# Rows for the expert blocks: four quarter gathers a block against one whole gather with a trip through DRAM

## The chip, the cores and the metric

The kernel runs on one core of one Trainium2 chip. The metric is the device time of one execution in microseconds (us), the median of the runs shown. Durations inside the kernel come from one profiled execution; times within it count from the start of its span.

The engines are named as in the profile: PE (TensorE; its weight loads are PEld), DVE (VectorE), ACT (ScalarE), POOL (GpSimd) and SP (SyncE, which here only starts DMAs).

## The reference, cut to what matters

Input x is 8 x 256 rows of 512 numbers, 2048 rows in all. A first layer (layer norm, a long convolution by head, a weighting with `ctx_2048`, a residual) yields a new x. The second layer is a mixture of experts, and the change is in how it gets its rows:

```
xf = layernorm(x).reshape(2048, 512)
scores = sigmoid(xf @ gate_w.T)                       # 8 experts
topk_w, topk_idx = top_k(scores, 2)
topk_w = topk_w / topk_w.sum() * 2.5
shared_out = (silu(xf @ shared_wg.T) * (xf @ shared_wu.T)) @ shared_wd.T
h = silu(xf @ exp_wg[e].T) * (xf @ exp_wu[e].T)       # 352 wide, per expert e
all_out[e] = h @ exp_wd[e].T
out = x + shared_out + sum over the 2 picked experts of topk_w * all_out[e]
```

Each row needs two experts of eight, so the kernel computes only those 4096 pairs of row and expert.

## The kernel before, in words

**First stage.** 16 tiles of 128 rows pass through the convolution (a loop over 32 pairs of heads). Beside it run the shared expert's products, as `steps` called one by one, and the routing by chunks of four tiles. The normed rows are stored to the DRAM tensor `xn_d` (L342). The residual tiles `x2` get the shared expert's output and go to `out` by SP (L757).

**Routing into a table.** For every chosen pair a row number and a gate are scattered to a table in DRAM, sorted by expert (L661). `load_table` brings it back as `tab` (L893). One-hot products on PE then pick out the table's column for each block: `slots` (L931) for whole blocks and `half_slots` (L948) for half blocks. Their results become the row numbers `row` (for scattering results), the gates `gate`, and the gather indices `src` and `src_h`.

**Blocks.** The pairs are cut into 34 blocks of 128 rows that always run: 26 "pure" ones of one expert, and 8 "mixed" ones whose two halves of 64 rows belong to two experts (from position 7 of the sequence on, every third). 16 further half blocks stand behind a branch (L1358, after block 6 is prepared) and do not run with these inputs.

For a block b, in order of its data:

- `gather(b)` (L1180) issues four indirect DMAs on POOL. DMA c fetches, for the 32 rows of chunk c, each row's four quarters of 128 numbers into four groups of 32 partitions of `xg`. So the quarters come to lie as `block_T` needs them. `xg` has four buffers.
- `block_T(b)` (L1213) is one transpose on DVE by 32x32 squares, `xg` to `xT`.
- `block_up` (L1257): PE multiplies by the expert's gate and up weights `wgu_sb` (loaded by SP at L1138); ACT and DVE form h.
- `block_hT` (L1300): transposes of 32-row pieces on DVE, 16 for each block, to `hTb`.
- `block_down` (L1315): PE multiplies by the down weights `wd_sb`; ACT scales by the gate into `ys` (three buffers, L1332), and POOL scatters the block with addition into `out` (`send`, L1336). A mixed block sends its first half at once; the second half is put into `late` and sent by `send_late` later. Sends add to the same tensor, so each waits until the one before has landed.

**Order.** The order is written by hand; every engine runs its instructions in program order. Gathers of the first four blocks are issued before the last four steps of the shared expert (L1229). Then the memory of the shared expert is released, and SP loads the down weights `wd_sb` into it (L1244, L1247), in two pieces for each of 8 experts; the first of these loads waits for the last stores of `x2`. PE's first down product needs expert 0's two pieces. In the main loop (L1368), turn k loads the expert number of block k+2, transposes block k+2, gathers block k+4, computes `block_up` and `block_hT` of block k and `block_down` of block k-2.

Around the table's return, two copies (L917) lay its columns out by quarters, on DVE and on ACT; the quarter products (L937, L955, L962) use them.

Of the kernel before, what the change touches and what calls it, by code (L numbers as in the profile page):

```python
# [8 lines left out]
F32 = mybir.dt.float32  # L9
I32 = mybir.dt.int32  # L10
AF = mybir.ActivationFunctionType
ALU = mybir.AluOpType
# [3 lines left out]
P = 128  # L16
B, D, L = 8, 256, 512
# [4 lines left out]
NTOK = NT * P  # L22
# [3 lines left out]
TC = TPC * P  # L26
# [24 lines left out]
HP = P // 2  # L51
# [18 lines left out]
def tile_xattn_moe(  # L70
# [29 lines left out]
    V, G, A, T, S = nc.vector, nc.gpsimd, nc.scalar, nc.tensor, nc.sync  # L100
# [63 lines left out]
    for e in range(NEXP):  # L164
# [6 lines left out]
        out=upper,  # L171
# [605 lines left out]
    def g(name, s, dtype=F32):  # L777
        return const.tile(s, dtype, name=name)
# [102 lines left out]
    def load_table():  # L881
# [20 lines left out]
                )  # L902
        return tab


    row = g("row", [P, NBLK + NMIX], I32)
    gate = g("gate", [P, NBLK])
    src = g("src", [P, NQ, NPURE], I32)
    src_h = [g(f"src_{n}", [P, 2, NHALF - n * NCOND], I32) for n in range(2)]
    by_quarter = []  # L910

    def turn_quarters(f, tab, copy):
        own = const.tile([P, TC], F32, name="rows_by_quarter") if f == 0 else shp.tile(
            [P, TC], F32, tag="sg", name="gates_by_quarter", bufs=2
        )
        by_quarter.append(own.rearrange("p (c q b) -> p c q b", c=NQ, q=NQ))
        copy(  # L917
            by_quarter[f],
            tab[:, :, f]
            .rearrange("p (c b) -> p c b", b=Q)  # L920
            .unsqueeze(2)
            .to_broadcast([P, NQ, NQ, Q]),
        )

    def lay_rows(to, ps, name, at=slice(0, P)):

        spare = g(name, [P, to.shape[1]])
        V.tensor_scalar(spare[at], ps, 0.0, lane[at], ALU.is_equal, ALU.mult)
        V.scalar_tensor_tensor(to, ps, float(NTOK), spare[at], ALU.add, ALU.add)

    def slots(tab, pick):  # L931

        ps = ps_tp.tile([P, 2 + NQ, NPURE], F32, tag="tp", name="slots_ps")
        for f in range(2):
            T.matmul(ps[:, f, :], lhsT=tab[:, :, f], rhs=pick, start=True, stop=True)
        for c in range(NQ):
            T.matmul(  # L937
                ps[:, 2 + c, :],
                lhsT=by_quarter[0][:, c].rearrange("p q b -> p (q b)"),
                rhs=pick,  # L940
                start=True,
                stop=True,
            )
        V.tensor_scalar(src, ps[:, 2:], float(NQ), behind, ALU.mult, ALU.add)
        lay_rows(row[:, :NPURE], ps[:, 0, :], "spare")
        V.tensor_copy(gate[:, :NPURE], ps[:, 1, :])

    def half_slots(any_half, first_half):  # L948

        ps = ps_tp.tile([P, 2, NQ, NHALF], F32, tag="tp", name="halves_ps")  # L950
        for f in range(2):
            quarter = [by_quarter[f][:, c].rearrange("p q b -> p (q b)") for c in range(NQ)]
            for c in range(2):
                for n in range(2):
                    T.matmul(  # L955
                        ps[:, f, c],
                        lhsT=quarter[2 * n + c],
                        rhs=any_half[:, n],
                        start=(n == 0),
                        stop=(n == 1),  # L960
                    )
                T.matmul(  # L962
                    ps[:, f, 2 + c, :NMIX],
                    lhsT=quarter[2 + c],
                    rhs=first_half,
                    start=True,
                    stop=True,
                )
        rows_h = g("rows_h", [P, NHALF])
        for n, m in enumerate((NHALF, NMIX)):  # L970
            two, cols = slice(2 * n, 2 * n + 2), slice(NPURE, NPURE + m)
            V.tensor_scalar(
                src_h[n], ps[:, 0, two, :m], float(NQ), behind, ALU.mult, ALU.add
            )
            for c in range(2):
                A.copy(rows_h[c * Q : (c + 1) * Q, :m], ps[c * Q : (c + 1) * Q, 0, 2 * n + c, :m])
                at = slice((2 * n + c) * Q, (2 * n + c + 1) * Q)
                A.copy(gate[at, cols], ps[at, 1, 2 * n + c, :m])
            at = slice(0, HP)
            to = slice(NPURE + n * NHALF, NPURE + n * NHALF + m)  # L980
            lay_rows(row[at, to], rows_h[at, :m], f"spare_{n}", at)


    def first_of_all(t):
# [33 lines left out]
    behind = const.tile([P, 1], F32, name="behind")  # L1018
    for q in range(NQ):
        G.memset(behind[q * Q : (q + 1) * Q], float(NTOK * NQ + q))  # L1020

    todo = iter(steps)
    done = 0
# [130 lines left out]
    settle()  # L1154
    for n in range(3):
        step()
        if n == 2:
            turn_quarters(0, tab, V.tensor_copy)
            turn_quarters(1, tab, A.copy)
        settle()  # L1160
    slots(tab, pick)
    half_slots(any_half, first_half)
# [8 lines left out]
    def send_late():  # L1171
        while late:
            send, *half = late.pop()
            send(*half)


    def rows_in(b):
        return P if b < NSURE else HP

    def gather(b):  # L1180
        xgs[b] = (rows if b < NSURE else spare).tile([P, NQ, P], F32, tag="xg", name=f"xg_{b}")
        for c in range(rows_in(b) // Q):
# [3 lines left out]
            G.indirect_dma_start(  # L1186
                out=xgs[b][:, c, :],
                out_offset=None,
                in_=xn_q,
                in_offset=bass.IndirectOffsetOnAxis(ap=at[:, c % at.shape[1], i : i + 1], axis=0),  # L1190
                bounds_check=(NTOK + P) * NQ - 1,
                oob_is_err=True,
            )

    def load_ek(b):
# [119 lines left out]
    def block_down(k):  # L1315
        if k < NSURE:
            ps = ps_b.tile([P, L], F32, tag="dn", name=f"y_{k}")
        else:
            ps = ps_spare.tile([P, 2, L], F32, tag="up", name=f"y_{k}")[:, 0]
        hT = hTb.pop(k)  # L1320
        for ft, (_, fw) in enumerate(F_TILES):
            for at, e in eks[k]:
                T.matmul(  # L1323
                    ps[at],
                    lhsT=hT[:fw, ft].rearrange("p c b -> p (c b)")[:, at],
                    rhs=weights(wd_sb, k, e, ft * L, L)[:fw],
                    start=(ft == 0),
                    stop=(ft == NF - 1),
                )
        y = (blk if k < NSURE else spare).tile([P, L], F32, tag="y", name=f"ys_{k}")  # L1330
        n = rows_in(k)
        A.activation(y[:n], ps[:n], AF.Copy, scale=gate[:n, k : k + 1])  # L1332


        def send(at, col):
            G.indirect_dma_start(  # L1336
                out=out,
                out_offset=bass.IndirectOffsetOnAxis(
                    ap=row[: at.stop - at.start, col : col + 1], axis=0
                ),  # L1340
                in_=y[at],
                in_offset=None,
                bounds_check=NTOK + P - 1,
                oob_is_err=True,
                compute_op=ALU.add,
            )

        send(eks[k][0][0], k)
        if len(eks[k]) > 1:
            late.append((send, slice(HP, P), k + NHALF))  # L1350

    more = nc.values_load(
        used[0:1, 0:1], min_val=2 * NPURE, max_val=2 * NPURE + NHALF,
# [122 lines left out]
```

## Time and profile before

| | us |
|---|---|
| median of 3 runs (806.08 to 808.03) | 807.78 |
| the profiled execution | 806.57 |
| its span | 804.9 |
| PE busy | 765.0 (95%) |
| DVE busy | 526.1 (65%) |
| POOL busy | 472.1 (59%) |
| ACT busy | 201.0 (25%) |
| table back in SBUF, first slot product | 485.5 |
| first up product of the blocks | 517.4 |
| first down product of the blocks | 531.7 |
| last product of PE ends | 781.4 |
| last send issued by POOL | 795.0 |

In the profile, a line of a timeline reads: start, duration, engine, line of the source, operation, output<-inputs, shapes, count; in brackets stands how long the engine sat idle before it, and what ended that. A line of the groups reads: count, then busy us and the mean ns of one, then idle us before them with the releasers. "issue" means that nothing the profile shows was waited for. In the slices, a digit is the busy share of 1/40 of the span in tenths. A matmul of 32-bit numbers appears twice in a count. A table of stages gives for each stretch its length, PE's busy time and number of matmuls, the granted clock of PE as a share of full speed, the DMA engines' share and GB/s.

### The profile page before, as it was taken

To read this page: it belongs to the slowest core of one execution; us is meant where nothing else is said; L and a number is where in the kernel's file an instruction comes from. 1 tells how busy PE (TensorE), PEld (TensorE's weight loads), DVE (VectorE), ACT (ScalarE), POOL (GpSimd) and SP (SyncE) were. 2 spreads that over 40 slices of the span, in tenths; PEclk is the share of its full clock that TensorE was granted. 3 is DMA by queue.
4 is the path that set the end of the run, shared out by engine and by line. 5 is a ranking of instruction groups with operands and counts; after the bars stand their busy time and mean duration, and the time that the engine had idled before them with its cause. 6 is when DMAs were issued, how large, how long until landed. Compare 5 with 4: busy or idle time off the path is not lost. (4 is left out here: it accounts for less than half of the span.)

```text
span 804.9 us, 8780 instructions
## 1 busy us (share of the span) xinstructions
PE 765.0 (95%) x2539; PEld 341.8 (42%) x2539; DVE 526.1 (65%) x1199; ACT 201.0 (25%) x387; POOL 472.1 (59%) x477
## 2 busy tenths in 40 slices
PE   9999999999999999999999998999999999999770
PEld 4333334433334433334434445455544544554330
DVE  3678868767558767658654372198877777676630
ACT  2222342543342543341422101011111111111110
POOL 7877785289175289175240035737677777777531
PEclk9999999999999999999999998999999999999895
DMA  7585433333504333412101951394333343334333
GB/s 248 181 286 168 151 117 118 117 47 111 170 33 125 117 46 112 138 33 92 52 14 59 416 178 44 109 298 83 60 60 69 64 67 62 58 70 67 59 40 39
DMA packets 51892, 88.13 MB, mean 109 GB/s; under 512 B 8832, under 2 KB 24192, under 8 KB 50688
## 3 DMA queue, kind: packets, MB, share of 16 engines
q1 hardware_dynamic: 37120, 61.77, 23.9%
q0 software_dynamic: 10400, 17.87, 12.9%
q10 hardware_dynamic: 4320, 7.87, 2.8%
q8 instruction: 24, 0.39, 0.2%
q14 instruction: 28, 0.23, 0.1%
HBM read 65.81 MB, written 21.66 MB: 109 GB/s over the span
## 5 line engine op out<-in xcount | busy, mean ns | idle before, releaser
L415 PE MATMUL cv<-kv,tz 128*64 128x512 f32 (+2 forms) x720 | 190.5, 607 | 0.2 <-POOL kv L375 0.2
L1186 POOL DMA_INDIRECT xg<-xn_d,src x136 | 138.6, 1019 | 55.5 <-issue 37.8
L1263 PE MATMUL up<-wgu_sb,xT 128*128 (+3 forms) x672 | 166.8, 460 | 3.1 <-DVE x L756 1.4
L687 PE MATMUL gu<-xfT,wsh 128*128 128x512 f32 x352 | 157.1, 600 | 1.2 <-issue 1.2
L375 POOL TENSOR_TENSOR kv<-vT,ctxT 128x512 f32<-128x512 f32 x128 | 133.1, 1073 | 18.4 <-issue 10.1
L1307 DVE STREAM_TRANSPOSE hTb<-h 32x96 f32<-32x96 f32 (+1 forms) x528 | 137.9, 261 | 7.9
L1263 PEld LDWEIGHTS up<-wgu_sb,xT 128*128 128x128 f32 (+1 forms) x672 | 97.0, 170 | 77.1 <-issue 33.4
L415 PEld LDWEIGHTS cv<-kv,tz 128*64 128x64 f32 (+2 forms) x720 | 60.9, 150 | 119.8 <-issue 97.8
L687 PEld LDWEIGHTS gu<-xfT,wsh 128*128 128x128 f32 x352 | 67.5, 193 | 85.8 <-issue 84.3
L1323 PE MATMUL y<-wd_sb,hTb 128*128 (+5 forms) x252 | 96.5, 608 | 6.8 <-DVE hTb L1307 5.4
L1336 POOL DMA_INDIRECT out_dram<-ys,row x42 | 65.5, 1560 | 63.5 <-issue 32.3
L477 DVE TENSOR_TENSOR prod<-cv,ctxT 128x1024 f32<-128x1024 f32 x64 | 78.2, 1221 | 16.4 <-PE cv L415 14.8
L661 POOL DMA_INDIRECT table<-entries,to x32 | 31.6, 987 | 90.5 <-DVE at L657 81.9
L486 DVE TENSOR_REDUCE convT<-prod 128x128 f32<-128x1024 f32 x64 | 78.1, 1220 | 2.2
L731 PE MATMUL dn<-wshd,hT 128*128 128x512 f32 x160 | 70.2, 593 | 0.0
L1323 PEld LDWEIGHTS y<-wd_sb,hTb 128*128 128x128 f32 (+3 forms) x252 | 35.8, 173 | 54.5 <-issue 43.3
L701 ACT ACTIVATE sg<-gu 128x512 f32<-128x512 f32 (+1 forms) x24 | 14.3, 596 | 162.8 <-PE gu L687 149.1
L531 POOL TENSOR_TENSOR skip<-ctxT,w 128x512 f32<-128x512 f32 x16 | 17.3, 1081 | 59.3 <-ACT w L523 30.1
L1332 ACT ACTIVATE ys<-y,gate 128x512 f32<-128x512 f32 x34 | 23.4, 687 | 109.4 <-DMA out_dram<-ys,row 62.4
L1271 ACT ACTIVATE h<-up 128x352 f32<-128x352 f32 x34 | 15.7, 463 | 138.1 <-PE up L1263 138.1
L415 PE MATMUL cv<-kv,td 128*128 128x512 f32 x88 | 47.2, 619 | 0.0
L1218 DVE STREAM_TRANSPOSE xT<-xg 128x512 f32<-128x512 f32 x34 | 24.1, 710 | 34.4 <-DMA xg<-xn_d,src 26.1
(188 smaller groups left out, 618.6 us busy)
## 6 DMA issues: line engine op xcount, KB each, us to landing
tz<-in_toep_dram SPq DMA_DIRECT2D x32, 384.0 KB, 3.4
wgu_sb<-in_egu_dram SPq DMA_DIRECT2D x8, 1408.0 KB, 15.4
ctxT<-in_cT_dram SPq DMA_DIRECT2D x16, 384.0 KB, 4.6
x<-in_xv_dram SPq DMA_DIRECT2D x16, 256.0 KB, 3.5
x<-in_x_dram SPq DMA_DIRECT2D x16, 256.0 KB, 4.7
xn_d<-xn ACTq DMA_DIRECT2D x16, 256.0 KB, 2.3
out_dram<-x SPq DMA_DIRECT2D x16, 256.0 KB, 2.5
wd_sb<-in_ed_dram SPq DMA_DIRECT2D x8, 512.0 KB, 10.0
```

The lines of the kernel that those rows point to most:

```text
L375: G.tensor_tensor(kv[:, mb], vT[t][:, at, :, cols].unsqueeze(2).to_broadcast([P, B, NH, NH]), ctxT[t][:, at, :, cols].unsqueeze(3).to_broa ...
L415: T.matmul(banks[lb][cols], lhsT=w, rhs=x, start=first, stop=left[lb][here[0]] == 0,)
L477: V.tensor_tensor(prod, ps.rearrange("p k b j i -> p (k b) j i"), ctxT[t][:, 2 + 2 * n : 4 + 2 * n, :, cols] .rearrange("p k b i -> p (k b ...
L486: V.tensor_reduce(convT[t][:, two, :, cols].rearrange("p k b j -> p (k b) j"), prod, AX.X, ALU.add)
L661: ins = G.indirect_dma_start(out=table, out_offset=bass.IndirectOffsetOnAxis(ap=to[:, i : i + 1], axis=0), in_=entry[:, i, n, :], in_offse ...
L687: T.matmul(ps, lhsT=wsh[:, k, m0 : m0 + m], rhs=rhs[k], start=(k == 0), stop=(k == NLB - 1))
L731: T.matmul(ps, lhsT=hTs[c][:, ft, i * P : (i + 1) * P], rhs=wshd[:, ft, :], start=(ft == 0), stop=False,)
L1186: G.indirect_dma_start(out=xgs[b][:, c, :], out_offset=None, in_=xn_q, in_offset=bass.IndirectOffsetOnAxis(ap=at[:, c % at.shape[1], i : i ...
L1263: T.matmul(ps[at, m, :FF], lhsT=xTs[k][:, j].rearrange("p c b -> p (c b)")[:, at], rhs=weights(wgu_sb, k, e, (m * NLB + j) * FF, FF), star ...
L1307: V.transpose(hT[q * Q : (q + 1) * Q, :n, c], hk[c * Q : (c + 1) * Q, q * NF * Q : (q * NF + n) * Q].rearrange("p (t a) -> p t a", a=Q),)
L1323: T.matmul(ps[at], lhsT=hT[:fw, ft].rearrange("p c b -> p (c b)")[:, at], rhs=weights(wd_sb, k, e, ft * L, L)[:fw], start=(ft == 0), stop= ...
L1336: G.indirect_dma_start(out=out, out_offset=bass.IndirectOffsetOnAxis(ap=row[: at.stop - at.start, col : col + 1], axis=0), in_=y[at], in_o ...
```

## The change

- `gather` issues one indirect DMA on POOL: 128 whole rows of 2 KB into a new SBUF tile `picked` (one buffer). SP then writes `picked` to a DRAM tile of its own, and brings it back into `xg` by four DMAs, one for each quarter. All five are on SP's queue.
- The gathers are issued two blocks earlier: three more before the down weights are loaded (one after each of three of the last four steps), and in the main loop turn k gathers block k+6, from turn 1 on.
- `send_late` is no longer called inside `gather`, only after it.
- The table is no longer laid out by quarters. The row numbers come from `tab` itself; the half blocks' products have 64 columns of the table as weights and write 64 partitions. `src`, `src_h`, `rows_h` and `behind` go; the second halves' row numbers get a tile of their own. `slots` has 2 products instead of 6, `half_slots` 7 instead of 12, and the 8 small ACT copies become copies on DVE.

The rest of the program and its order are the same. The diff, cut to what the text speaks of:

```diff
    def slots(tab, pick):
-    ps = ps_tp.tile([P, 2 + NQ, NPURE], F32, tag="tp", name="slots_ps")
+    ps = ps_tp.tile([P, 2, NPURE], F32, tag="tp", name="slots_ps")
     for f in range(2):
         T.matmul(ps[:, f, :], lhsT=tab[:, :, f], rhs=pick, start=True, stop=True)
-    for c in range(NQ):
-        T.matmul(
-            ps[:, 2 + c, :],
-            lhsT=by_quarter[0][:, c].rearrange("p q b -> p (q b)"),
-            rhs=pick,
-            start=True,
-            stop=True,
-        )
-    V.tensor_scalar(src, ps[:, 2:], float(NQ), behind, ALU.mult, ALU.add)
     lay_rows(row[:, :NPURE], ps[:, 0, :], "spare")
     V.tensor_copy(gate[:, :NPURE], ps[:, 1, :])
...
+    halves = [slice(n * HP, (n + 1) * HP) for n in range(2)]
+    for f in range(2):
+        for n in range(2):
+            T.matmul(
+                ps[halves[0], f],
+                lhsT=tab[:, halves[n], f],
+                rhs=any_half[:, n],
+                start=(n == 0),
+                stop=(n == 1),
+            )
+    for at, f, to in ((1, 0, 0), (1, 1, 1), (0, 0, 2)):
         T.matmul(
+            ps[halves[at], to, :NMIX],
+            lhsT=tab[:, halves[1], f],
+            rhs=first_half,
             start=True,
             stop=True,
         )
...
-        if n == 2:
-            turn_quarters(0, tab, V.tensor_copy)
-            turn_quarters(1, tab, A.copy)
...
    def gather(b):
-    xgs[b] = (rows if b < NSURE else spare).tile([P, NQ, P], F32, tag="xg", name=f"xg_{b}")
-    for c in range(rows_in(b) // Q):
-        if c == 3:
-            send_late()
-        at, i = (src, b) if b < NPURE else (src_h[c // 2], b - NPURE)
-        G.indirect_dma_start(
-            out=xgs[b][:, c, :],
-            out_offset=None,
-            in_=xn_q,
-            in_offset=bass.IndirectOffsetOnAxis(ap=at[:, c % at.shape[1], i : i + 1], axis=0),
-            bounds_check=(NTOK + P) * NQ - 1,
-            oob_is_err=True,
-        )
+    n = rows_in(b)
+    own = rows if b < NSURE else spare
+    picked = own.tile([P, L], F32, tag="picked", name=f"picked_{b}", bufs=1)
+    G.indirect_dma_start(
+        out=picked[:n],
+        out_offset=None,
+        in_=xn_d,
+        in_offset=bass.IndirectOffsetOnAxis(ap=row[:n, b : b + 1], axis=0),
+        bounds_check=NTOK + P - 1,
+        oob_is_err=True,
+    )
+    picked_d = dram.tile([n, L], F32, name=f"picked_d_{b}")
+    S.dma_start(out=picked_d, in_=picked[:n])
+    xgs[b] = own.tile([P, NQ, P], F32, tag="xg", name=f"xg_{b}")
+    for q in range(NQ):
+        S.dma_start(
+            out=xgs[b][q * Q : (q + 1) * Q, : n // Q],
+            in_=picked_d[:, q * P : (q + 1) * P].rearrange("(c b) m -> b c m", b=Q),
+        )
...
 for k in range(TPC):
     step()
     settle()
     if k <= AHEAD:
         block_T(seq[k])
+        gather(seq[k + AHEAD + 2])
...
-        if k + AHEAD + 2 < NSURE:
-            gather(seq[k + AHEAD + 2])
+        if 0 < k < NSURE - AHEAD - 4:
+            gather(seq[k + AHEAD + 4])
         send_late()
```

More of the change, by code (lines that the diff above doesn't have):

```diff
@@ L903, in load_table @@
         return tab
-    row = g("row", [P, NBLK + NMIX], I32)
+    row = g("row", [P, NBLK], I32)
+    second_row = g("second_row", [HP, NMIX], I32)
     gate = g("gate", [P, NBLK])
[L908 to L914, printed above, removed]
-        )
[L916 to L922, printed above, removed]
-        )
     def lay_rows(to, ps, name, at=slice(0, P)):
@@ L931, in slots, with half_slots @@
     def slots(tab, pick):
-        ps = ps_tp.tile([P, 2 + NQ, NPURE], F32, tag="tp", name="slots_ps")
+        ps = ps_tp.tile([P, 2, NPURE], F32, tag="tp", name="slots_ps")
         for f in range(2):
             T.matmul(ps[:, f, :], lhsT=tab[:, :, f], rhs=pick, start=True, stop=True)
-        for c in range(NQ):
+        lay_rows(row[:, :NPURE], ps[:, 0, :], "spare")
+        V.tensor_copy(gate[:, :NPURE], ps[:, 1, :])
+    def half_slots(any_half, first_half):
+        ps = ps_tp.tile([P, 3, NHALF], F32, tag="tp", name="halves_ps")
+        halves = [slice(n * HP, (n + 1) * HP) for n in range(2)]
[9 more added lines that the diff above has]
+        for at, f, to in ((1, 0, 0), (1, 1, 1), (0, 0, 2)):
             T.matmul(
-                ps[:, 2 + c, :],
-                lhsT=by_quarter[0][:, c].rearrange("p q b -> p (q b)"),
-                rhs=pick,
+                ps[halves[at], to, :NMIX],
+                lhsT=tab[:, halves[1], f],
+                rhs=first_half,
                 start=True,
@@ L943, in slots @@
             )
-        V.tensor_scalar(src, ps[:, 2:], float(NQ), behind, ALU.mult, ALU.add)
[L945 to L954, printed above, removed]
-                    T.matmul(
[L956 to L965, printed above, removed]
-                    start=True,
-                    stop=True,
-                )
-        rows_h = g("rows_h", [P, NHALF])
-        for n, m in enumerate((NHALF, NMIX)):
[L971 to L981, printed above, removed]
+        for n, m in enumerate((NHALF, NMIX)):
+            at, cols = halves[n], slice(NPURE, NPURE + m)
+            lay_rows(row[at, cols], ps[at, 0, :m], f"spare_{n}", at)
+            V.tensor_copy(gate[at, cols], ps[at, 1, :m])
+        lay_rows(second_row, ps[halves[0], 2, :NMIX], "spare_2", halves[0])
     def first_of_all(t):
@@ L1016, in tile_xattn_moe @@
     G.memset(first_block[:, 0:1], float(P - 1))
-    behind = const.tile([P, 1], F32, name="behind")
-    for q in range(NQ):
-        G.memset(behind[q * Q : (q + 1) * Q], float(NTOK * NQ + q))
     todo = iter(steps)
@@ L1332, in block_down, with send @@
         A.activation(y[:n], ps[:n], AF.Copy, scale=gate[:n, k : k + 1])
-        def send(at, col):
+        def send(at, index, col):
             G.indirect_dma_start(
@@ L1338, in send @@
                 out_offset=bass.IndirectOffsetOnAxis(
-                    ap=row[: at.stop - at.start, col : col + 1], axis=0
+                    ap=index[: at.stop - at.start, col : col + 1], axis=0
                 ),
@@ L1346, in send @@
             )
-        send(eks[k][0][0], k)
+        send(eks[k][0][0], row, k)
         if len(eks[k]) > 1:
-            late.append((send, slice(HP, P), k + NHALF))
+            late.append((send, slice(HP, P), second_row, k - NPURE))
     more = nc.values_load(
```

## The prediction

> **What bounds the kernel now.** I read the page first (slices, costliest groups), then the timelines of PE, POOL and SP from 480 us on, the clock by stage, and the order of instructions in both programs. TensorE is busy 765.0 of 804.9 us; that hides that in the blocks' stage POOL sets the pace.
>
> ```profile
> PE   9999999999999999999999998999999999999770
> POOL 7877785289175289175240035737677777777531
> ...
> L1186 POOL DMA_INDIRECT xg<-xn_d,src x136 | 138.6, 1019 | 55.5 <-issue 37.8
> L1336 POOL DMA_INDIRECT out_dram<-ys,row x42 | 65.5, 1560 | 63.5 <-issue 32.3
> ```
>
> A tenth of 7 on POOL looks like slack. POOL's timeline at the end shows that it is none: the gaps between its DMAs are the 0.30 us that follows every one of them.
>
> ```profile
> 751.36 1.60 POOL L1336 DMA_INDIRECT out_dram<-ys,row  x1 [1.77 <-issue]
> 753.27 1.05 POOL L1186 DMA_INDIRECT xg<-xn_d,src  x1 [0.31 <-DVE h L1275]
> 754.63 1.00 POOL L1186 DMA_INDIRECT xg<-xn_d,src  x1 [0.31 <-issue]
> 755.94 1.01 POOL L1186 DMA_INDIRECT xg<-xn_d,src  x1 [0.31 <-issue]
> 757.25 1.01 POOL L1186 DMA_INDIRECT xg<-xn_d,src  x1 [0.30 <-issue]
> ...
> 764.18 1.45 POOL L1336 DMA_INDIRECT out_dram<-ys,row  x1 [3.99 <-ACT ys L1332]
> 768.15 1.43 POOL L1336 DMA_INDIRECT out_dram<-ys,row  x1 [2.52 <-DMA out_dram<-ys,row]
> 772.60 1.56 POOL L1336 DMA_INDIRECT out_dram<-ys,row  x1 [3.02 <-DMA out_dram<-ys,row]
> ...
> 789.41 1.56 POOL L1336 DMA_INDIRECT out_dram<-ys,row  x1 [4.03 <-DMA out_dram<-ys,row]
> 794.98 1.56 POOL L1336 DMA_INDIRECT out_dram<-ys,row  x1 [4.01 <-issue]
> ```
>
> Three blocks (two whole, one mixed with two sends) take POOL 24.8 us (sends at 726.57 and 751.36), PE 22.3 (up at 623.81 and 646.10). POOL falls 2.5 us behind in every three. Each send also waits for the one before to land: 5.57 us apart with 128 rows, 4.2 on average with 64 (764.18, 768.15, 772.60). So the last send starts at 794.98 though PE is done at 781.4, and the span ends 9.9 us after that send. PE pays too:
>
> ```profile
> 531.73 2.74 PE L1323 MATMUL y<-wd_sb,hTb 128*128 128x512 f32 x6
> ...
> 749.42 2.74 PE L1323 MATMUL y<-wd_sb,hTb 128*128 x6
> 757.60 4.61 PE L1323 MATMUL y<-wd_sb,hTb 128*128 x6 [5.43 <-DVE hTb L1307]
> ```
>
> DVE waits for a late gather, hTb is late, PE stands 5.43 us and then runs at half clock (4.61 for 2.74). With 1.05 and 0.23 us of waits a little earlier, POOL's lag costs PE 5.43 + 1.87 + 1.28 = 8.6 us.
>
> The other place is SP's queue before the blocks:
>
> ```profile
> 506.99 10.74 SPq L757 DMA_DIRECT2D out_dram<-x  x4
> 521.02 0.40 SPq L1244 DMA_DIRECT2D wd_sb<-in_ed_dram  x1
> ```
>
> The down weights (wd) start once the last residual store has landed, 3.6 us after its issue at 517.4. The first expert's two pieces need 4.8 more (the second goes out 0.5 later, 4.3 us minimum to landing), so at 525.8 they are there; PE wants them at 531.73. Slack: 6 us.
>
> **The change, part by part.**
>
> *Table stage.* Gone: the two 128x512 copies, the quarter products, the 8 small ACT copies. 18 products become 9: 485.50 to 490.81 now, 9 at 0.23 us (slots_ps to its quarters: 0.47 for two) is 2.1, so 3.2 us less on PE. The granted clock (column after PE's busy time and count) is half here, after 2.4 us of idling and these tiny products:
>
> ```profile
> 488.00:489.00 1.00, 1.00 (x8) 0.58 0.00 0
> ...
> 495.00:496.00 1.00, 1.00 (x4) 1.00 0.01 0
> ```
>
> If it stays full, up to 5.4 us are saved; if the same stretch stays slow, 2.1. I take 3.7. PE would reach the first down product at 528.0. The row numbers are ready at 486.7 (tab 485.45, two products, two DVE operations) instead of 487.7.
>
> *The gathers on POOL.* 136 become 34. At 1.31 us with their gap, three a block are gone: 3.9 us of 8.2 per block. A 2 KB-row gather is in no row; on POOL it lies between 1.01 (quarter) and 1.56 (the send, same shape). Either leaves POOL well below PE.
>
> *The trip.* Each block now goes gather, write to DRAM, four reads, and there is one buffer `picked`, so the next gather waits for this write. Cycle c = gather + write + about 0.2 of hand-over. The write has a twin: ACT's store of xn and SP's reads of it follow by 2.06 us (419.58 to 421.64). The gather's landing lies between 2.6 us (64 KB quarter) and 4.8 (send, 256 KB read, added and written). I take 3.6, nearer the quarter because nothing is added: c = 5.9, bounds 4.9 and 7.1 (estimates from these rows). Four reads take SP 1.75 to issue and 3.3 to land.
> [...]
>
> *What queues behind it on SP.* Five blocks' trips stand ahead of the first two residual stores, seven ahead of wd. Gather 6's write lands at 486.7 + 7c; reads and stores issue to x15 2.2, landing and wait 3.6, first expert 4.8: PE gets wd at 497.3 + 7c = **538.6**, against 531.7 before. PE stands from 528.0 to 538.6, so all of the table stage's saving is spent waiting. The wait brings half clock: the trace's case (757.6 to 761.9 slow, so 4.3 us at half speed) costs 2.1. PE is **9.0 us late** here. Bounds: c 4.9 gives 531.6 (+2.0 with slow clock), c 7.1 gives 547.0 (+17.4).
> [...]
>
> *First blocks after it.* wd's 16 issues are held to 13.9 us (521.0 to 534.9), so block 7's write issues at 547.7 and lands like wd's pieces, 10.1 later: 557.8. POOL is in order: gather 8 waits for that write, and send 0 stands behind gather 8, at 559.3; its result is ready at 544.1. Lag 15 us. ys has three buffers: ys 3 needs send 0 landed (564.7), y 3 ends at 565.5, so PE does not feel it. DVE transposes xg 7 (landed 561.4) when hT 4 is done, about 561. Then POOL gains: with c at 6.4 beside the sends, three blocks take 6.4 + 6.4 + 7.4 (late send: 1.3 + 4.2 + 1.9) = 20.2 against PE's 22.3. Seven whole blocks first win 7 x (7.3 - 6.4) = 6.4, the branch at block 6 drains the queues and loses some 4.6 (POOL's wait before its send at 570.9), six triples win 6 x 2.1 = 12.6. Lag 15 - 6.4 + 4.6 - 12.6 = about 0 by the end.
>
> *The end.* With POOL on time PE's 8.6 us go. PE ends at 781.4 + 9.0 - 8.6 = 781.8. The last send follows the one before it by 5.57: 1.9 us after PE's end instead of 13.6: 783.7. Plus 9.9: **span 793.6**, 11.3 less. The profiled execution took 806.57 with span 804.9 (1.7 around it), and lies 1.2 under the median of 807.78: 793.6 + 1.7 + 1.2 = 796.5, forecast **797**.
>
> **Rivals.**
> 1. *The trip is slower than a block* (slower). For: single buffer, in-order POOL and SP, gathers sharing the software queue with sends. Against: quiet rows sum to 5.9. It decides from c = 7.5, where three cycles reach PE's 22.3 and the lag never closes. Send 25 is then at 559.3 + 4 + 25 x 7.5 = 751, the ten sends after it take 50 (six at 5.57, four at 4.2): 801, span 811, time **814**; with 7.5 in the head as well (11 us later) 825.
> 2. *The gather lands like a quarter*: c 4.9. For: size hardly shows in quiet rows, where SP's 64 KB reads and ACT's 256 KB stores both land in 2.0 to 2.3 us. PE ends at 781.4 + 2.0 - 8.6 = 774.8, last send 776.7, time **789.5**.
> 3. *Gain and stall cancel*: c about 6.7 in the head (wd at 544.2, PE 14.6 late) with 3 us of send lag left. PE ends 787.4, last send 792.3, time **805**: no change.
> 4. *The change doesn't do what it says*: against it, the program has one 128x512 gather a block and five SP transfers; under 0.02.
>
> **Chances.** Forecast 0.54 (its own range 791 to 804), rival 2 0.15, rival 3 0.11, rival 1 0.20. A measurement of this kernel can tell about 0.3%, 2.4 us, from no change. Rival 3 splits: 0.03 faster, 0.06 the same, 0.02 slower. Faster 0.72, same 0.06, slower 0.22. The range reaches from rival 2 without its 2.1 us of slow clock (787) into rival 1 (814); some 0.05 lies below, 0.12 above.
>
> **What would show it.** Right: PE waits some 10 us at its first down product for a DMA of wd; wd's first issue near 534 on SP; gathers 5.9 us apart in the head; POOL no longer busy through; no PE wait at 750; last send under 4 us after PE's last product. Wrong: gathers over 7.5 us apart in the blocks' stage, DVE waiting for xg there, or a last send far behind PE (rival 1); a first down product before 533 (rival 2).

## The result and the profile after

The changed kernel took **817.97 us** (median of 4 runs, 816.82 to 822.92) against 807.9 of the kernel before beside it: ratio 1.0137, 95% interval 1.0089 to 1.0185. It is slower, and the forecast of 797 and its range up to 814 were wrong. The profiled execution took 816.82, with a span of 815.1. One later run of the changed kernel (run 6) took 1139.25 us at a granted clock of 0.653; it is in no median here.

The page of the changed kernel, two rows of the slices and the two POOL groups that answer to those shown before (the eight sends of second halves, by `second_row`, are now a group of their own):

```profile
PE   9999999999999999999999989839999999999960
...
POOL 7877876298256297257220221102233434343331
...
L1145 POOL DMA_INDIRECT picked<-xn_d,row x34 | 36.0, 1059 | 144.0 <-DMA picked_d<-picked 119.0
L1304 POOL DMA_INDIRECT out_dram<-ys,row x34 | 52.7, 1549 | 82.4 <-DMA out_dram<-ys,row 41.9
```

POOL works about half as much in the blocks' stage (3 and 4 where 7 stood), just as wanted. But it is not free: it stood 119.0 us ahead of its gathers, 86.0 of them from 553 us on, waiting for the write of `picked` to DRAM. A busy share does not show this; the column behind the bar does.

Where PE lost time, from PE's timeline of the changed kernel:

```profile
513.00 14.47 PE L1231 MATMUL up<-wgu_sb,xT 128*128 128x352 f32 x48 [1.39 <-DVE x L756]
542.32 4.41 PE L1291 MATMUL y<-wd_sb,hTb 128*128 128x512 f32 x6 [14.85 <-DMA wd_sb<-in_ed_dram]
546.56 4.90 PE L1231 MATMUL up<-wgu_sb,xT 128*128 x16
...
780.20 4.51 PE L1291 MATMUL y<-wd_sb,hTb 128*128 x6 [2.21 <-DVE hTb L1275]
784.54 0.49 PE L1263 MATMUL hT_ps<-ident,hp 128*128 128x128 f32 x3
788.58 5.49 PE L1291 MATMUL y<-wd_sb,hTb 128*128 x6 [3.55 <-ACT hTb L1264]
```

PE comes to the blocks 4.4 us earlier (513.00, before 517.43), then stands 14.85 us at its first down product and runs that one at the slow clock (4.41 instead of 2.74; the granted clock is 0.50 up to 545). And the waits at the end are still there. POOL's timeline shows why; first and last sends, and two sends three blocks apart:

```profile
559.60 1.01 POOL L1145 DMA_INDIRECT picked<-xn_d,row  x1 [25.59 <-DMA picked_d<-picked]
560.91 1.62 POOL L1304 DMA_INDIRECT out_dram<-ys,row  x1 [0.30 <-issue]
...
645.74 1.46 POOL L1304 DMA_INDIRECT out_dram<-ys,second_row  x1 [0.30 <-issue]
...
668.61 1.46 POOL L1304 DMA_INDIRECT out_dram<-ys,second_row  x1 [0.30 <-issue]
...
754.41 1.46 POOL L1304 DMA_INDIRECT out_dram<-ys,row  x1 [0.54 <-ACT ys L1300]
...
799.35 1.56 POOL L1304 DMA_INDIRECT out_dram<-ys,row  x1 [4.10 <-DMA out_dram<-ys,row]
804.81 1.55 POOL L1304 DMA_INDIRECT out_dram<-ys,row  x1 [3.91 <-DMA out_dram<-ys,row]
```

Send 0 starts at 560.91, 25.4 us later than before (535.48). From 645.74 to 668.61 POOL needs 22.9 us for three blocks; PE needs 22.3. So the lag does not close, and the last send starts 10.7 us after PE is done at 794.07. From send 0 to the last it is 243.9 us, where before had 259.5: the stage did become 15.6 shorter, and starts 25.4 later.

One cycle of the trip in the quiet head, POOL and SP of the changed kernel:

```profile
493.11 1.03 POOL L1145 DMA_INDIRECT picked<-xn_d,row  x1 [5.17 <-DMA picked_d<-picked]
499.74 1.01 POOL L1145 DMA_INDIRECT picked<-xn_d,row  x1 [5.61 <-DMA picked_d<-picked]
```

```profile
496.73 0.34 SPq L1154 DMA_DIRECT2D picked_d<-picked  x1
...
538.47 0.39 SPq L1212 DMA_DIRECT2D wd_sb<-in_ed_dram  x1
...
551.28 0.34 SPq L1154 DMA_DIRECT2D picked_d<-picked  x1
558.91 1.75 SPq L1157 DMA_DIRECT2D xg<-picked_d  x4
```

Gather at 493.11, its write at 496.73, the next gather at 499.74. Seven of these put wd's first issue to 538.47. Block 7's write, behind wd's sixteen issues, goes at 551.28 and is landed at 558.91; gather 8 waits for it, and send 0 for gather 8.

### The profile page after: what moved, and what is told of

It is laid out like the page before. It is cut to its first block, busy times and chain, and to the rows that moved or that the text cites. A ratio compares the mean times of both kernels' runs of the same rounds, so it can differ in the third digit from the quotient of the medians.

```text
span 815.1 us, 8765 instructions
## 1 busy us (share of the span) xinstructions
PE 764.0 (94%) x2521; PEld 337.7 (41%) x2521; DVE 527.1 (65%) x1199; ACT 198.0 (24%) x378; POOL 368.0 (45%) x371
## 2 busy tenths in 40 slices
DMA packets 74741, 105.97 MB, mean 130 GB/s; under 512 B 9920, under 2 KB 42688, under 8 KB 73536
## 4 chain that ended last, share of the span: by engine, by line
PE 52%; DMA 33%; issue 7%; DVE 3%; POOL 1%; SPq 1%; POOLq 1%; ACT 1%; ACTq 0%; DVEq 0%
PE cv L415 24%; PE gu L687 16%; DMA picked<-xn_d,row 13%; DMA picked_d<-picked 9%; PE dn L731 6%; DMA out_dram<-ys,row 4%; DMA out_dram<-ys,second_row 4%; PE same L446 2%; DMA table<-entries,to 1%; DMA wd_sb<-in_ed_dram 1%; PE ptr L547 1%; PE dn L744 1%; DMA xn_d<-xn 1%; DVE prod L477 1%; DVE convT L486 1%
## 5 line engine op out<-in xcount | busy, mean ns | idle before, releaser
L1291 PE MATMUL y<-wd_sb,hTb 128*128 (+5 forms) x252 | 100.8, 626 | 21.1 <-DMA wd_sb<-in_ed_dram 14.9
L1145 POOL DMA_INDIRECT picked<-xn_d,row x34 | 36.0, 1059 | 144.0 <-DMA picked_d<-picked 119.0
L1304 POOL DMA_INDIRECT out_dram<-ys,row x34 | 52.7, 1549 | 82.4 <-DMA out_dram<-ys,row 41.9
L1240 DVE TENSOR_TENSOR h<-h,up 128x352 f32<-128x352 f32 x34 | 17.1, 502 | 53.1 <-ACT h L1239 50.3
L731 PEld LDWEIGHTS dn<-wshd,hT 128*128 128x128 f32 x160 | 30.2, 190 | 37.6 <-issue 37.6
```

The costliest lines, as they stand in the source:

```text
L731: T.matmul(ps, lhsT=hTs[c][:, ft, i * P : (i + 1) * P], rhs=wshd[:, ft, :], start=(ft == 0), stop=False,)
L1145: G.indirect_dma_start(out=picked[:n], out_offset=None, in_=xn_d, in_offset=bass.IndirectOffsetOnAxis(ap=row[:n, b : b + 1], axis=0), boun ...
L1291: T.matmul(ps[at], lhsT=hT[:fw, ft].rearrange("p c b -> p (c b)")[:, at], rhs=weights(wd_sb, k, e, ft * L, L)[:fw], start=(ft == 0), stop= ...
L1304: G.indirect_dma_start(out=out, out_offset=bass.IndirectOffsetOnAxis(ap=index[: at.stop - at.start, col : col + 1], axis=0), in_=y[at], in ...
```

## The experiments

**Theory 1**: POOL's in-order chain (gather, write, next gather, with the sends between) sets the end. It starts late, because SP's queue holds block 7's write behind wd, and its cycle is no shorter than PE's block. **Theory 2**: PE's wait for wd (14.9 us and 1.7 of slow clock) is the loss, the rest is harmless. **Theory 3**: the sends, each waiting for the one before to land, are the bound whatever the trip does.

The kernel before took 818.8, 819.3 and 818.3 us beside the first three sets of four runs, and 807.0 beside the last. The changed kernel differed less (818.0, 821.3, 820.9 on three chips), so its variants are read against it. It was not run beside runs 1 to 4 and 9 to 12, so a difference of 3 us there shows nothing. The difference in the kernel before is taken up at runs 5, 9, 13 and 14.

**1. wd among the trips.** The head's three further gathers go behind the first three experts' weights:

```diff
     if k <= AHEAD:
         block_T(seq[k])
-        gather(seq[k + AHEAD + 2])
...
     S.dma_start(out=wde[: FF - 2 * P, 2, :], in_=ed[e, 2 * P : FF])
+    if e < AHEAD + 1:
+        gather(seq[e + AHEAD + 2])
```

> The three gathers of the head's last steps are moved behind the first three experts' down weights (wd), so four trips instead of seven stand ahead of wd's first issue; everything else is as in the changed kernel. Theory 1 (POOL's chain of gather, write, next gather sets the end; it starts when block 7's write gets through SP's queue behind wd): wd comes at about 497.3 + 4 x 6.6 = 523.7 and PE does not stand at its first down product, but block 7's write still stands behind wd's sixteen issues, send 0 still starts between 553 and 566, and PE soon stands for a buffer of ys instead. Time 811 to 823, as the changed kernel. Theory 2 (the 14.9 us that PE stands at its first down product, with 1.7 of slow clock, are the loss): 818.0 - 16.6 = 801, range 798 to 804. Theory 3 (the sends, each waiting for the landing of the one before, are the bound): send 0 follows the first result, at about 531, and the end moves with it by 25 us or more: 790.

Measured 817.61 (816.21 to 819.09). PE's timeline has no wait at the first down product, and POOL's starts and ends where the changed kernel's does:

```profile
525.33 2.74 PE L1292 MATMUL y<-wd_sb,hTb 128*128 128x512 f32 x6
```

```profile
561.68 1.62 POOL L1305 DMA_INDIRECT out_dram<-ys,row  x1 [0.30 <-issue]
...
805.85 1.55 POOL L1305 DMA_INDIRECT out_dram<-ys,row  x1 [3.68 <-DMA out_dram<-ys,row]
```

PE reaches that product 17 us earlier and the end does not move: theory 2 falls. PE gives the time back further on, 6.54 us at the branch and 0.4 to 2.0 at four waits for `ys`.

**2. Two buffers for the picked rows**, the trip itself unchanged:

```diff
-rows = pool("rows", 4)
+rows = pool("rows", 5)
...
-    picked = own.tile([P, L], F32, tag="picked", name=f"picked_{b}", bufs=1)
+    picked = own.tile([P, L], F32, tag="xg", name=f"picked_{b}")
...
-        gather(seq[k + AHEAD + 4])
+        gather(seq[k + AHEAD + 3])
```

> The picked rows get two buffers in turn with xg (five buffers of one tag, where before there were four of xg and one of picked), so gather b+1 does not wait for the write of b; gathers are issued one block later than in the changed kernel, six ahead of wd. The trip through DRAM and its bytes stay. Theory 1: a trip costs SP's order alone, write landing 2.06 + reads 1.75 + next write 0.34 and a little, some 4.4 us instead of 6.6; the first down product does not wait (wd there at about 522, PE at 527), send 0 follows its result at about 533, three blocks take POOL less than PE's 22.3, and no lag is left: PE ends at 781.4 - 4.4 (table stage) - 8.6 (before's waits by lag) = 768, the last send 2 us later, span 780, time 783, range 779 to 791. Theory 2: 818.0 - 16.6 = 801, range 798 to 804. Theory 3: the chain of sends keeps its 243.9 us from 533 on, last send 777, time 790. Were the bytes of the trip the cause, it would stay above 810.

Measured 788.83 (786.19 to 790.13), 29 us less than the changed kernel with the same bytes and transfers. It takes no more memory: the four buffers of `xg` and the one of `picked` became five that both use in turn. The edit also issues each gather one block later, so the 29 us are not the buffers' alone; run 7, which also puts each send one gather earlier, prices such a shift at 4.5. Send 0 starts at 533.80, the last at 778.07, 3.4 after PE's end:

```profile
778.07 1.56 POOL L1304 DMA_INDIRECT out_dram<-ys,row  x1 [3.92 <-DMA out_dram<-ys,row]
```

Of theory 1's 783, 5.8 are missing: PE waits 1.45 for wd and then 0.99, 0.34 and 2.08 for h, with slow clock (6.55 us for the up products at 573.45, 4.90 elsewhere), because trips from block 6 on stand behind wd (runs 8 and 12). Theory 3's 790 is as near (from send 0 to the last it is 244.3 us, as theory 3 has it), so this run alone does not part the two.

**3. Two buffers, and wd late again**:

```diff
+idle = dram.tile([P, P], F32, name="idle")
+for n in range(5):
+    S.dma_start(out=idle, in_=ones)
+    S.dma_start(out=ones, in_=idle)
 wd_pool = pool("wd", reuse_waits="tile")
```

> As the run with two buffers for the picked rows, but with five round trips of 64 KB (to DRAM and back, each waiting for the other) put into SP's queue ahead of wd, so that wd is about as late as in the changed kernel: first issue between 533 and 542. It leaves no work out; the added transfers write back what they read. Theory 1: the head costs PE the same wait as in the changed kernel, but with a fast trip the lag of the sends closes in the blocks, so the waits of the last blocks (0.5 + 2.2 + 3.6 and slow clock) and most of the 10.7 us from PE's end to the last send go: PE ends at about 787, last send 789, time 802, range 798 to 808. Theory 2 (the wait for wd is the whole loss, whatever the trip does in the blocks): 818, range 814 to 822. Theory 3 (the sends' chain): it starts as late as in the changed kernel, 818.

Measured 801.62 (799.59 to 802.86). PE stands 13.71 us for wd (its first down product at 542.78, the changed kernel's 542.32), yet this is 16 us faster, so the wait for wd is not the whole loss. Theory 1 said 802, theory 2 818. Against theory 3 it says less than meant: gathers are issued one block later here, so send 0 stands ahead of gather 8 (550.71) and started at 548.78, not at 561. A chain of 243.9 from there would have put the time at about 806; it took 238.9.

**4. No trip**:

```diff
-    out=picked[:n],
+    out=xgs[b][:n].rearrange("p c m -> p (c m)"),
...
-picked_d = dram.tile([n, L], F32, name=f"picked_d_{b}")
-S.dma_start(out=picked_d, in_=picked[:n])
...
```

> The gather writes whole rows straight into xg; the write to DRAM and the four reads are left out, and with them the laying out by quarters, so each block's transposes see their rows in another layout (that part of the computation is changed). It prices everything that the trip costs. Theory 1: as without lag, PE's end at 768 or some us before, time 783, range 779 to 788. Theory 2: 801, range 798 to 804. Theory 3: 790.

Measured 781.78 (779.91 to 782.93), against theory 1's 783. Theory 3's 790 is too long: from send 0 to the last it is 237.4 us here.

**5 and 6. Both kernels again**, unchanged, on another chip.

> The kernel before, unchanged, on the chip of this group of runs, so that the times of this group have their own base: 806 to 810, granted clock about 0.979 over the span, last send near 795. If it comes out near 818, chips differ by more than the kernels do, and only ratios within a group may be read.

> The changed kernel, unchanged, on the same chip: 816 to 820, granted clock about 0.971, send 0 near 561 and the last send near 805. Theory 1 asks that its chain on POOL be the same again: three blocks in 22.5 to 24.2 us, no shorter than PE's 22.3.

Measured 818.87 and 821.33 (817.96 to 825.14; ratio of the changed one to before there 1.0029, 0.9992 to 1.0067: no difference that can be told). The changed kernel's chain is the same (send 0 at 561.47, three blocks in 23.9 us from 649.37 on, last send 809.43). The kernel before is 11 us slower than at first. DVE's timeline of run 5 shows where:

```profile
507.60 1.29 DVE L1218 STREAM_TRANSPOSE xT<-xg 128x512 f32<-128x512 f32 x2
527.38 1.29 DVE L756 TENSOR_TENSOR x<-dn,x 128x512 f32<-128x512 f32 x2 [18.49 <-remote]
```

The product that this add waits for was done at 516.0; in the first profile the add came at 516.09. DVE stood another 11.3 us; the trace names what ended that only as "remote". PE stood 12.56 us behind it at its first up product (1.39 in the first profile).

**7. Send before gather** in each turn of the loop, otherwise the changed kernel:

```diff
-    if 0 < k < NSURE - AHEAD - 4:
-        gather(seq[k + AHEAD + 4])
     send_late()
...
     if 2 <= k < last - 1:
         block_down(seq[k - 2])
...
+    if 0 < k < NSURE - AHEAD - 4:
+        gather(seq[k + AHEAD + 4])
```

> In the main loop the gather is issued behind the turn's send instead of ahead of it; nothing else differs from the changed kernel, so wd is as late and the trip as slow as there. Theory 1 (POOL's in-order chain of gather, write, next gather): send 0 no longer stands behind gather 8 and its wait for block 7's write, and each send comes one gather earlier, so the whole chain of sends moves up by one cycle of 7.6 us: last send 797, time 810, range 807 to 814. Theory 2 (PE's wait for wd): no change, 818. Theory 3 (the sends' own landing): send 0 at 546, the end 15 us earlier, 803. Were the wait for the gathers to push DVE's transposes late instead, it would be slower than 818.

Measured 816.78 (810.70 to 820.04), 4.5 below the changed kernel beside it (821.33; the ratios to before, 0.9937 to 0.9990 and 0.9992 to 1.0067, just part). That is outside theory 1's 807 to 814: the time gained less than the cycle it asked for. In the two profiles the last send moved by 7.0 (809.43 to 802.45), about one cycle; that is one profile of each. It did not move by the 14 by which send 0 itself did (547.26), so the sends' chain did not keep its length (255.2 us), and theory 3 falls as stated. Its chain would also be shorter than what was measured: two whole and two half sends at the spacing of the end before (5.57 and 4.2) take 19.5 us in three blocks, an estimate, where POOL takes 22.9. Landings do set the changed kernel's last ten sends: POOL stands 2.5 to 4.1 us ahead of each, for nine of them put down to the landing before.

**8. Two buffers, wd spread between the trips**: expert 0 behind five trips, expert 1 behind six, the others one in each turn.

```diff
+load_wd(0)
+gather(seq[2 * AHEAD + 1])
+load_wd(1)
...
     if 0 < k < NSURE - AHEAD - 3:
         gather(seq[k + AHEAD + 3])
+    if 0 < k < NEXP - 1:
+        load_wd(k + 1)
```

> Two buffers for the picked rows, as in the run with them, and wd in pieces between the trips: expert 0 behind five trips, expert 1 behind six, and expert k+1 behind the trip of turn k (1 to 6), each well ahead of the block that needs it. Theory 1: no wait for wd (two buffers alone left 1.5 us), and trips 6 to 10 no longer stand behind fourteen pieces of wd, so PE's waits of 1.0 + 0.3 + 2.1 us and its slow clock at 555 to 580 go, 6 us in all: 788.8 - 6 = 783, range 780 to 787, last send about 3 us after PE's end. If the trips still collide with wd's bytes wherever they stand, 787 to 790.

Measured 788.16 (786.61 to 793.22): no gain over run 2 that can be told, and not theory 1's 780 to 787. The wait for wd went, but waits of 1.05 (h) and 2.29 (xg) took its place: on SP each trip waits 4.4 to 5.9 us for its write to land beside a piece of wd, so trips were 7.3 to 9.7 us apart there.

**9. The kernel before, with a pause in POOL's gathers**:

```diff
-    if k + AHEAD + 2 < NSURE:
+    if k + AHEAD + 2 < NSURE and k not in (1, 2):
         gather(seq[k + AHEAD + 2])
...
+    if k == 2:
+        gather(seq[k + AHEAD + 1])
+        gather(seq[k + AHEAD + 2])
```

> The kernel before, with the gathers of blocks 5 and 6 issued behind send 0 instead of ahead of it, so that POOL pauses from about 514 to 531. In the unchanged kernel's run of the second group DVE stands 11.3 us at the add of residual tile 14 (from PE's product at 516.0 to 527.4, 3.0 us after the last of POOL's back-to-back gathers), which the first profile of the kernel before does not show. If that stand goes with the gathers on POOL, the add comes at about 516, wd's first issue near 521, PE's first up product at 517.5, and the time is 808 to 812 on any chip. If it has nothing to do with them, the add stays near 527 and the time at 818 or above, for the gathers are a little later.

Measured 815.66 (before there 818.26). The add came at 516.94, without the stand, but later gathers cost PE 6.26 us at the branch, and the time fell by 2.6 only. The add's place fits the first answer, the time neither; that this chip has the stand at all is only read from its 818.26.

**10. The table stage's work put back** into the changed kernel:

```diff
     step()
+    if n == 2:
+        turn_quarters(0, tab, V.tensor_copy)
+        turn_quarters(1, tab, A.copy)
...
+for n in range(9):
+    T.matmul(
+        ps[:, n],
+        lhsT=by_quarter[n // 5][:, n % NQ].rearrange("p q b -> p (q b)"),
+        rhs=pick,
+        start=True,
+        stop=True,
+    )
```

> The changed kernel with nine more small products and the two 128x512 copies put back ahead of the shared expert's last steps (their results are not used). Theory 1: PE loses 3 to 5 us before its first down product and waits as much less for wd, which hangs on the trips and not on PE; the gathers start with the row numbers, up to 1 us later. Time as the changed kernel's, within 1.5 us: 817 to 823. If the table stage's saving had come through to the end, 3.7 us more: 821.7 to 826.5.

Measured 820.70 (818.66 to 827.11), within the changed kernel's own spread (816.8 to 825.1 on three chips); the time alone cannot part the two answers, which lie 3.7 apart. The profile does: PE came to the blocks 4.4 later (517.36) and waited 3.2 less for wd (11.63). Most of what the table stage saves is waited away, as predicted, and the sends, which set the end, start where they did (562.84; 560.91 to 562.97 in the changed kernel).

**11. No sends**:

```diff
-    send(eks[k][0][0], row, k)
-    if len(eks[k]) > 1:
-        late.append((send, slice(HP, P), second_row, k - NPURE))
+    if k == seq[0]:
+        send(eks[k][0][0], row, k)
```

> The changed kernel with all sends but the first left out, so that the experts' results of the other blocks are not added to the output. It measures a trip in the blocks' stage alone. If the sends in flight make the trip longer there (7.6 us against the head's 6.6): gathers 6.6 to 6.9 us apart while they wait for the write before, no lag, PE ends near 787 with no wait after its first down product but the branch's, time 791, range 788 to 795. If the trip is as long without them, the spacing stays at 7.4 to 7.7 and PE waits for xg late in the stage: time 795 to 805.

Measured 787.52 (786.18 to 788.52). Gathers are 6.75 us apart from block 9 to 33, where the changed kernel has 7.69; the two ends of that row:

```profile
567.64 1.08 POOL L1145 DMA_INDIRECT picked<-xn_d,row  x1 [5.88 <-DMA picked_d<-picked]
...
729.60 1.01 POOL L1145 DMA_INDIRECT picked<-xn_d,row  x1 [5.95 <-DMA picked_d<-picked]
```

Worked out from POOL's and SP's starts:

| us | predicted | head | blocks | blocks, no sends |
|---|---|---|---|---|
| gather to its write | 3.6 | 3.71 | 3.97 | 3.84 |
| write to its reads | 2.06 | 2.14 | 2.68 | 2.21 |
| reads to the next gather | 0.2 | 0.74 | 1.04 | 0.70 |
| cycle | 5.9 (6.4 in the blocks) | 6.59 | 7.69 | 6.75 |

The sends make the cycle 0.9 longer: 0.6 in the two transfers, and 0.3 between a landed write and the next gather, where POOL has sends to issue in order (up to 2.12 there, 0.75 without sends). Of the time, 19 us are the sends behind PE's end, which are simply not there; PE's own end moved from 794.07 to 783.09. Without the sends, and with the same late wd, PE has no wait left but 0.45 at the branch and 0.77 in the last block.

**12 and 16. Reads behind the next gather**: run 8, with each block's reads placed behind the next block's gather, and gathers issued one block further ahead (turn k gathers block k+6, in run 8 block k+5) in the same five buffers.

```diff
+    def ahead(k):
+        if k < NSURE:
+            pick_rows(seq[k])
+        if k - 1 < NSURE:
+            bring(seq[k - 1])
...
     if 0 < k < NSURE - AHEAD - 3:
-        gather(seq[k + AHEAD + 3])
+        ahead(k + AHEAD + 4)
     if 0 < k < NEXP - 1:
         load_wd(k + 1)
+    if k > 0:
+        ahead_put(k + AHEAD + 4)
```

> As the run with wd spread between the trips, and on SP's queue each block's reads stand behind the next block's gather but ahead of its write, so SP no longer waits for a write to land before it reads; gathers run one block further ahead, five buffers for picked and xg as there. Theory 1: the waits left there (1.05 for h and 2.29 for xg, with 2.5 us of slow clock, where trips 5 to 12 were 7.6 to 9.7 us apart beside wd) go, 4 to 6 us: 788.2 - 5 = 783, range 780 to 786, a little above the 781.8 of the kernel without the trip. If the trips' bytes and not SP's waits hold them up beside wd, 786 to 790.

> The version with five buffers, wd between the trips and reads behind the next gather, again, beside both kernels on one chip: 777 to 783, 4 to 5% faster than either kernel if those have 818 to 823.

Measured 779.21 (778.48 to 781.09; 780 to 786 was expected), and 782.87 on the last chip. **It beats both kernels**: ratio to the kernel before 0.9528 (0.9512 to 0.9544) on the one chip, and 0.9686 (0.9655 to 0.9718) on the other, where before took 807. PE's timeline has three waits left after the table stage; the last product and the last send:

```profile
763.48 2.84 PE L1329 MATMUL y<-wd_sb,hTb 128*128 x6 [0.76 <-ACT hTb L1302]
```

```profile
763.44 1.56 POOL L1342 DMA_INDIRECT out_dram<-ys,row  x1 [4.03 <-ACT hTb L1302]
769.06 1.55 POOL L1342 DMA_INDIRECT out_dram<-ys,row  x1 [4.06 <-DMA out_dram<-ys,row]
```

The last send follows PE's end by 2.7 us, much as the prediction wanted it (1.9). But the reason given beforehand does not hold. In the loop SP's queue still has a block's reads right behind its write, as in run 8, and SP still waits for the landing:

```profile
528.11 0.38 SPq L1160 DMA_DIRECT2D picked_d<-picked  x1
532.46 1.77 SPq L1169 DMA_DIRECT2D xg<-picked_d  x4
```

From 515 to 598 us, 43.0 us pass in 11 such places between a write's issue and its reads (run 8: 39.5 in 9), and beside wd the writes of blocks 6 to 12 are 6.1 to 10.3 us apart. Only the first three blocks' reads come behind the next write. What did change is how early the trips start: for blocks 5 to 12 the write goes out 26.5 to 31.8 us ahead of PE's up product of that block, in run 8 16.7 to 27.1. That the lead is the cause fits the waits that went; no run varies it alone.

**13, 14 and 15. The kernel before, the same with only block 6's gather moved, and the changed kernel**, on the last chip.

> The kernel before, unchanged, beside the next three on one chip. If DVE's stand at the add of residual tile 14 belongs to the first group's chip alone being without it: the add at 527 again, PE waits 12.6 us at its first up product, time 817 to 821. Without the stand: add at 516, time 806 to 810.

> The kernel before with only block 6's gather issued behind send 0, so that POOL's row of gathers ends at about 519 instead of 524. If DVE's stand lasts until that row ends (3.0 us after its last gather's end in the earlier run), the add of residual tile 14 comes at about 522 and PE starts its up products 5.3 us earlier than in the unchanged kernel beside it. If the stand has a fixed length or another cause, the add stays near 527. If there is no stand, 516.

> The changed kernel, unchanged, on the same chip: no stand of DVE (its gathers on POOL are 6.5 us apart there), send 0 at 561, last send 805 to 810, time 817 to 823; against the kernel before with the stand 0 to 0.7% slower, without it 1 to 1.6%.

Measured 807.42, 811.97 and 820.85. The add in run 13 starts at 517.82, right after its product: no stand on this chip. So run 14 could not tell what ends it. Its 4.6 us fit one gather moved later in a stage that POOL bounds: PE waits 0.9 to 1.2 us for `h` in four places where run 13 has no such wait. The changed kernel against before here: 1.0146 (1.0104 to 1.0189), as in the first result.

## Why the prediction was wrong

Its span of 793.6 was 21.5 us short. By its own steps, from the timelines: the head 3.3 (PE 12.3 late at its second up product where 9.0 stood), PE's waits by lag 9.0 (its end at 794.07 and not 781.8, for the waits were said to go), the last send 8.8 (10.7 after PE's end, not 1.9), and 0.4 in what follows it.

- **Table stage**: right. 4.4 us saved (3.7 said), all waited away at the first down product; run 10 bears it out.
- **The gathers on POOL**: right. 1.06 us each (1.01 to 1.56 said).
- **The trip's cycle**: this term was mis-sized. "Gather 3.6 + write 2.06 + about 0.2 of hand-over" had its two transfers right and its hand-over wrong: from a landed write to the next gather on POOL 0.74 passes. So c was 6.59 in the head, not 5.9. Seven of them would be 4.8 later; the formula's other terms came out 1.1 shorter and the slow clock 0.4, which leaves the 3.3.
- **What queues behind it on SP**: right in kind. By its formula 497.3 + 7 x 6.59 is 543.4; PE started at 542.32. The slow clock cost 1.7 (2.1 said).
- **First blocks**: send 0 at 560.91 (559.3 said), and its reason, block 7's write behind wd, is what the trace shows. That the time came so close is luck: the write went out 3.6 later than said and landed in 7.6 us where 10.1 was said.
- **"Then POOL gains"**: the step that failed. c was said to be 6.4 beside the sends (7.4 with a late send, 6.7 on average) and three blocks 20.2; they are 7.69 and 22.9. The gain of 2.1 us a triple became a loss of 0.6, and the lag that the text closed was still there at the end. The mis-sized terms, in the blocks: hand-over 1.04 for 0.2, write 2.68 for 2.06, gather 3.97 for 3.6, together 1.8, where the 6.4 allowed 0.5 for the sends. Run 11 puts what the sends add at 0.9; the rest was there without them.
- **The end**: follows from that. The "8.6 us" of PE's waits were said to go because POOL would be on time; it was not.

Rival 1 was the case that happened, with its mechanism, its place and its threshold of 7.5. It had send 25 at 751 and 50 us for the ten sends after it; they are 754.41 and 50.4. Given 0.20 it was priced too low: the forecast's c of 6.4 lay 1.1 under the threshold, on a sum of three terms, none of which a row had measured in this stage. And the range ended at the rival's time with a quiet head (814), though its text named 825 with a slow head as well; the result lies between.

The gather's 3.6 was an estimate between two rows, 2.6 and 4.8; the head shows 3.4 to 4.2 from issue to the write that waits for it. The write stood at 2.04 to 2.41 there (2.06 said). The three parts are paid one behind the other: 3.71, 2.14 and 0.74 make the head's 6.59.

What was not shown is why DVE stands 11.3 us in the kernel before on one chip (two more have its slow time, without a profile) and not on two others. It does not touch the changed kernel, whose time is the same on three chips within 0.4%, but it decides whether the change loses 1.4% or nothing that can be told (0.3%).

## What to carry to other kernels

Where an engine in order waits for a transfer that another queue has to start, the busy time saved on it says little (here POOL's fell from 472.1 to 368.0 us, and the time rose by 1.4%): write down the whole cycle with the hand-overs and the sharing of buffers, and compare it with the consumer's period. Here five buffers used in turn instead of four and one, with gathers one block later, were worth 29 us, where moving the waits about gave 0 (run 1) and 4.5 (run 7). And look at how early a trip starts in a queue that runs in order: spreading wd alone (run 8) gained nothing that can be told, and with trips one block further ahead (run 12) the ratio to the kernel before went from 0.9639 to 0.9528, though no run varies that lead alone.

## What the runs showed of the hardware that was not expected

- From a write's landing to POOL's next gather 0.74 us pass in the head (0.70 to 0.78), and 0.70 in the blocks without sends, measured from SP's issue that the same landing releases.
- With scatters with addition in flight a plain 256 KB write to DRAM takes 2.68 us on average until its reads are issued, at most 4.81 (2.67 and 2.61 in runs 6 and 15); without them (run 11) 2.21, at most 3.18.
- In the kernel before on one chip DVE stood 11.3 us with its product done, while POOL issued gathers every 1.31 us, and went on 3.0 us after the last of them had been issued. Each of those gathers takes POOL 1.0 us, so no single one spans the 11.3. On two other chips the same program has no such stand. The cause was not shown.
- The trip through DRAM, 17.8 MB more (105.97 against 88.13), costs nothing that can be told in runs 12 and 16, where the trips start early (in run 12, for blocks 5 to 12, 26.5 to 31.8 us ahead of the up product): 779.2 and 782.9 with it, 781.8 without (run 4), on three different chips.
